# First MLP stage of a transformer block: the last 64 features added by passes of 512 columns over two sums at a time

## The chip, the cores and the metric

The kernel runs on one core of a Trainium2 chip. Its engines work side by side and wait for each other by semaphores: TensorE (PE in the profile; PEld is its weight load) multiplies into the accumulation memory PSUM, VectorE (DVE), ScalarE (ACT) and GpSimd (POOL) work on tiles of 128 partitions, SyncE (SP) issues DMAs. Each engine takes its own instructions in order. The metric is the time of one execution on the device in microseconds; the median of several runs is given.

## The reference

One transformer block with conditioning, two sequences of 2048 tokens with 576 features. The change is in the first product of the MLP, `xn2 @ w1`, and what feeds it.

```python
mod = silu(c) @ w_ada + b_ada
sh_msa, sc_msa, g_msa, sh_mlp, sc_mlp, g_mlp = split(mod, 6, axis=1)
xn = _ln(x, 1e-06) * (1 + sc_msa[:, None, :]) + sh_msa[:, None, :]
q, k, v = heads_of(xn @ w_qkv + b_qkv)          # 16 heads of 36
attn = softmax(einsum('bqhd,bkhd->bhqk', _ln(q), _ln(k)) * 36 ** -0.5)
x = x + g_msa[:, None, :] * (merge(attn @ v) @ w_proj + b_proj)
xn2 = _ln(x, 1e-06) * (1 + sc_mlp[:, None, :]) + sh_mlp[:, None, :]
h = gelu(xn2 @ w1 + b1)                          # 576 -> 2304, exact gelu
out = x + g_mlp[:, None, :] * (h @ w2 + b2)
```

All inputs and outputs are float32.

## The kernel before

The program goes through input products, attention, output products, the first MLP stage, and the second MLP stage. The change is in the first MLP stage and in the preparation of its operands, which is laid between the output products just ahead of it.

The stage works on the 4096 tokens in 8 blocks (`n`) of 512, and on the 2304 hidden features in 9 pairs (`f`) of chunks of 128, one chunk of the left half and one of the right half of `w1`. That makes 72 jobs, numbered job = 9n + f, done two at a time (an even job and the odd one after it). Even jobs use PSUM side 0, odd ones side 1, so a job can begin only when the sums of the job two before it have been read.

Of the 576 features the first 512 are multiplied by a scheme of seven products instead of eight: tokens (two halves t0 and t1 of 256), features (two halves of 256) and hidden chunks (left and right) form a 2 x 2 by 2 x 2 product. `whole_part` issues the seven products m1 to m7 of a job, each two matmuls of 256 columns in float32, which the hardware runs as two passes each: 28 passes. `token_sums` makes the four sums of token parts that the scheme needs, once a block, on VectorE; `weight_sums` makes those of the weights. Six products stand two to a bank in the three PSUM banks of a side (in the order 4, 2, 6, 3, 5, 7), m1 in a bank that the sides share. `hidden_made` combines them: ScalarE copies m1, VectorE does four additions (lines 2121, 2124, 2127, 2128), ScalarE the gelu, GpSimd four sums that the second stage wants, and a DMA stores them.

The last 64 features do not fit the scheme. `last_part` adds them by passes in float32r (one pass instead of two), for which both operands are split into a high part and a rest: the weight tile `wr` has the high parts of 64 rows in partitions 0 to 63 and the rests in 64 to 127, the token tile `parts` has the rows repeated, high in slot 0 and rest in slot 1. Left columns times t0 go to m2, right minus left times t1 to m4, right times t1 to m7, right times t0 to m3: four targets by two slots are eight matmuls of 256 columns a job. `wr` holds three weights: left, right, right minus left.

The token tiles of a block come by DMA from a transposed copy (`turned_loaded`), and ScalarE applies the modulation in place (`turned_modulated`): four operations for the 512 features, then `last_modulated`, which writes the high part (line 393) and the full value into a scratch tile `tail` (line 394), from which GpSimd makes the rest (line 395). `ahead(job)` places this work for the next block between the jobs: tile i of block m+1 is modulated at job 9m + 2i + 2, so its last tile (i = 3) at job 9m + 8. Two tiles of the block after it are normalised and turned at the jobs around it (statistics on lines 277 and 279, turn on line 1042), on VectorE too.

The order on the engines is that of the program text: VectorE, ScalarE, GpSimd, SP and TensorE are told to keep it. In the loop over pairs of jobs it is

```python
ahead(job); whole_part(n0, f0, 0)
if f1 == 0: token_sums(n1)
last_part(n0, f0, 0); ahead(job + 1); hidden_made(n0, f0, 0)
whole_part(n1, f1, 1); last_part(n1, f1, 1)
if f1 == HF - 1 and n1 + 1 < NB: token_sums(n1 + 1)
hidden_made(n1, f1, 1)
```

So where a block begins on an odd job (9, 27, 45, 63) its token sums stand ahead of the additions of the job before, and where it begins on an even job (18, 36, 54) behind those of two jobs before.

Of the kernel before, what the change touches and what calls it, by code (L numbers as in the profile page):

```python
# [12 lines left out]
ALU = mybir.AluOpType  # L13
# [18 lines left out]
def dit_block(  # L32
# [724 lines left out]
    def block_of_small():  # L757
# [294 lines left out]
        def turned_loaded(dst, cols, turned, queue):  # L1052

            full, parts, _ = dst
            queue.dma_start(out=full[:, :, cols], in_=turned[0:512, :].rearrange("(k p) n -> p k n", p=P))
            for r0 in (0, 64):
                queue.dma_start(out=parts[r0 : r0 + 64, 1, cols].bitcast(F32), in_=turned[512:576, :])

        def turned_modulated(dst, cols, which, b):

            full, parts, _ = dst
            for k in range(FULL):
                part = full[:, k, cols]
                nc.scalar.activation(part, part, AF.Identity, **affine(which, k, b))  # L1064
            last_modulated(dst, cols, parts[:, 1, cols].bitcast(F32), which, b)
# [741 lines left out]
        for b in range(B):  # L1807
# [101 lines left out]
            if b + 1 < B:  # L1909
# [68 lines left out]
        wr = [mw.tile([P, MH], F32R, name=f"wr{i}") for i in range(3)]  # L1978
# [14 lines left out]
        for j in range(TPB + 1):  # L1993
            n, t = divmod(j, TPB)
            turned_loaded(xnts[n], slice(t * P, (t + 1) * P), opening["turned"][j], nc.sync)
# [27 lines left out]
        for j in range(TPB + 1):  # L2023
            n, i = divmod(j, TPB)
            due(2 * j + 5, lambda n=n, i=i: turned_modulated(xnts[n], slice(i * P, (i + 1) * P), 2, 0))
# [43 lines left out]
        def sums_of(side):  # L2069

            flat = ps_m[side].rearrange("p b c -> p (b c)")
            return {m: flat[:, i * PAIR : (i + 1) * PAIR] for i, m in enumerate((4, 2, 6, 3, 5, 7))} | {
                1: ps_m1[:, side, :]
            }

        def whole_part(n, f, side):


            a = xnts[n % 2][0]
            t = [slice(0, PAIR), slice(PAIR, BLK)]  # L2080
            moving = {
                1: lambda k: a[:, k, t[0]],
                2: lambda k: a[:, 2 + k, t[0]],
                3: lambda k: ss[4][:, k, :],
                4: lambda k: a[:, 2 + k, t[1]],
                5: lambda k: ss[1][:, k, :],
                6: lambda k: ss[2][:, k, :],
                7: lambda k: a[:, k, t[1]],
            }
            out_m = sums_of(side)  # L2090

            for m in (2, 4, 1, 5, 6, 7, 3) if n == f == 0 else (2, 4, 5, 6, 7, 3, 1):
                for k in range(2):
                    nc.tensor.matmul(  # L2094
                        out_m[m],
                        wb[:, f, slot[m], k, :],
                        moving[m](k),
                        start=k == 0 and m in (1, 2, 5, 6),
                        stop=k == 1 and m == 1,
                    )  # L2100

        def last_part(n, f, side):
            a = xnts[n % 2][1]
            out_m = sums_of(side)

            for m, w, t in ((2, 0, 0), (4, 2, 1), (7, 1, 1), (3, 1, 0)):
                for i in range(2):
                    nc.tensor.matmul(  # L2108
                        out_m[m],
                        wr[w][:, f * P : (f + 1) * P],  # L2110
                        a[:, i, t * PAIR : (t + 1) * PAIR],
                        start=False,
                        stop=i == 1 and m != 2,
                    )

        def hidden_made(n, f, side):
            cs = css[(n * HF + f) % 3]
            flat = ps_m[side].rearrange("p b c -> p (b c)")
            two = lambda i: flat[:, i * PAIR : (i + 2) * PAIR].rearrange("p (a c) -> p a c", a=2)
            nc.scalar.copy(cs[:, 4, :], ps_m1[:, side, :])  # L2120
            nc.vector.tensor_tensor(  # L2121
                cs[:, 0:5:4, :], two(1), cs[:, 4:5, :].to_broadcast([P, 2, PAIR]), ALU.add
            )
            nc.vector.tensor_tensor(
                cs[:, 2:4, :], two(4), cs[:, 4:5, :].to_broadcast([P, 2, PAIR]), ALU.add
            )
            nc.vector.tensor_tensor(cs[:, 1, :], cs[:, 3, :], flat[:, 0:PAIR], ALU.subtract)  # L2127
            nc.vector.tensor_tensor(cs[:, 2:4, :], cs[:, 2:4, :], two(3), ALU.add)  # L2128
# [15 lines left out]
        def ahead(job):  # L2144
# [11 lines left out]
            for what, todo in at(read=0, turn=-2, load=-5, modulate=2):  # L2156
                m, i = todo
                block, cols = xnts[m % 2], slice(i * P, (i + 1) * P)
# [4 lines left out]
                elif what == "read":  # L2163
                    turned_loaded(block, cols, rows_ahead.pop(todo), nc.sync)
                else:
                    turned_modulated(block, cols, 2, m // NBLK)
# [356 lines left out]
```

## Time and profile before

| | |
|---|---|
| median of 3 runs | 3066.44 us (3065.35 to 3068.48) |
| profiled execution | 3067.53 us |
| its span, first to last instruction | 3065.5 us |
| PE busy | 3037.7 us (99%) |
| DVE busy | 1702.6 us (56%) |
| ACT busy | 1497.7 us (49%) |
| POOL busy | 1000.9 us (33%) |
| first MLP stage | from 2112.6 to about 2620 us |

The profile is one execution. Busy time of TensorE is modelled and pipelined, so the rate of its passes is read from start to start in the timeline, not from the mean duration of a record. The share of busy time is an average over stages; the stage of the change has to be read by itself.

### The profile page before, as it was taken

The page shows a single profiled execution, that of the slowest core. Times are in us where ns is not written, and L with a number is a line of the kernel's source. Part 1 is how long each engine was busy: PE and PEld are TensorE (multiplying, and loading weights), DVE is VectorE, ACT ScalarE, POOL GpSimd, SP SyncE. Part 2 cuts the span into 40 slices and gives each one's busy share as a digit, 9 for nine tenths or more (in the row PEclk, how much of TensorE's full clock was granted, in tenths as well). Part 3 has the DMA queues.
Part 4 walks back from the last instruction along what each step waited for, and adds up shares of the span by engine and source line. Part 5 has one row for each costly group of instructions (what it writes and reads, how often), then busy time and mean ns, then how long its engine had stood idle before and what let it go on. Part 6 is the DMA issues. An engine that isn't in the chain of part 4 may idle for free.

```text
span 3065.5 us, 51337 instructions
## 1 busy us (share of the span) xinstructions
PE 3037.7 (99%) x19015; PEld 1891.3 (62%) x19015; DVE 1702.6 (56%) x2614; ACT 1497.7 (49%) x2921; POOL 1000.9 (33%) x1263
## 2 busy tenths in 40 slices
PE   8999999999999999999999999999999999999999
PEld 5884333333333688633333333347888888999999
DVE  6773455444553566544444444447766664667766
ACT  2326666766666223466666666643655553000000
POOL 4651100123222445301101111115545554545444
PEclk9999999999999999999999999999999999999999
DMA  5873322333333454412222222236887887855554
GB/s 146 190 146 93 102 68 71 79 92 93 93 88 94 164 128 81 95 43 69 52 54 72 62 69 66 77 92 191 249 239 238 247 240 279 317 197 193 200 192 157
DMA packets 427939, 415.17 MB, mean 135 GB/s; under 512 B 231472, under 2 KB 355920, under 8 KB 419552
## 3 DMA queue, kind: packets, MB, share of 16 engines
q1 hardware_dynamic: 390824, 314.46, 34.6%
q0 software_dynamic: 36848, 97.33, 11.7%
q8 instruction: 153, 2.51, 0.3%
q14 instruction: 106, 0.87, 0.1%
q10 hardware_dynamic: 8, 0.00, 0.0%
HBM read 246.43 MB, written 154.75 MB: 131 GB/s over the span
## 4 chain that ended last, share of the span: by engine, by line
PE 97%; DVE 1%; DMA 1%; ACT 1%; issue 0%; SPq 0%; POOL 0%; DVEq 0%; ACTq 0%
PE b L1549 30%; PE b L1536 20%; PE b L2353 12%; PE m L2094 11%; PE s L1143 7%; PE s L1229 5%; PE s L1717 4%; PE m L2108 2%; PE one L2094 2%; PE b L2362 2%; PE s L1145 1%; PE s L1235 1%; PE s L1714 1%; DMA xt<-in_x_dram 0%; PE b L197 0%
## 5 line engine op out<-in xcount | busy, mean ns | idle before, releaser
L1540 ACT ACTIVATE pt<-b 128x512 f32<-128x512 f32 x2048 | 1057.4, 608 | 481.7 <-PE b L1549 267.4
L1549 PE MATMUL b<-pt,vt 128*64 128x512 f32 x4096 | 935.0, 598 | 1.8 <-ACT pt L1540 1.8
L1549 PEld LDWEIGHTS b<-pt,vt 128*64 128x64 f32 x4096 | 271.8, 136 | 583.9 <-issue 438.0
L1536 PE MATMUL b<-qm,km 32*128 32x512 f32 x4096 | 563.6, 613 | 0.0
L1605 DVE TENSOR_TENSOR ot<-b,ot 128x512 f32<-128x512 f32 x186 | 128.6, 692 | 549.7 <-PE b L1549 549.7
L1536 PE MATMUL b<-qe,ke 16*128 16x512 f32 x2048 | 420.0, 791 | 0.0
L1536 PEld LDWEIGHTS b<-qm,km 32*128 32x128 f32 x4096 | 190.5, 184 | 271.2 <-ACT pt L1540 210.0
L1143 PE MATMUL s<-wq,xnt 128*128 128x288 f32 x864 | 226.9, 406 | 2.3 <-ACT xnt L400 2.0
L2370 ACT COPY one<-b 128x144 f32<-128x144 f32 x55 | 15.3, 279 | 405.9 <-PE b L2353 405.9
L2094 PE MATMUL m<-xnt,wb 128*128 128x256 f32 x864 | 210.4, 379 | 3.1 <-DVE cs L2128 1.8
L2094 PE MATMUL m<-s,wb 128*128 128x256 f32 x864 | 210.0, 379 | 0.0
L1570 DVE RECIPROCAL den<-den 128x512 f32<-128x512 f32 x62 | 206.8, 3336 | 0.0
L1603 DVE COPY ot<-b 128x512 f32<-128x512 f32 x62 | 42.9, 692 | 262.4 <-PE b L1549 262.4
L1143 PEld LDWEIGHTS s<-wq,xnt 128*128 128x128 f32 x864 | 157.7, 190 | 38.1 <-ACT xnt L400 2.7
L2094 PEld LDWEIGHTS m<-s,wb 128*128 128x128 f32 x864 | 164.2, 190 | 22.4
L1536 PEld LDWEIGHTS b<-qe,ke 16*128 16x128 f32 x2048 | 106.6, 184 | 113.9 <-issue 113.2
L2094 PEld LDWEIGHTS m<-xnt,wb 128*128 128x128 f32 x864 | 158.8, 190 | 23.1 <-DVE cs L2128 2.4
L2132 ACT ACTIVATE cs<-cs,b_sb 128x512 f32<-128x512 f32 x144 | 100.5, 721 | 140.8 <-DVE cs L2127 140.7
L1793 POOL DMA_DIRECT2D spare<-in_x_dram x32 | 17.8, 556 | 453.2 <-DVE met L796 453.2
L2134 POOL TENSOR_TENSOR cs<-cs 128x256 f32<-128x256 f32 x72 | 60.7, 844 | 244.2 <-ACT cs L2132 244.2
L1064 ACT ACTIVATE xnt<-xnt,mod 128x128 f32<-128x128 f32 x244 | 100.0, 481 | 52.7 <-DMA xnt<-turned 45.7
L2121 DVE TENSOR_TENSOR cs<-m,cs 128x512 f32<-128x512 f32 x72 | 49.4, 686 | 136.3 <-PE m L2108 82.4
(369 smaller groups left out, 4583.9 us busy)
## 6 DMA issues: line engine op xcount, KB each, us to landing
operands<-cs SPq DMA_DIRECT2D x70, 896.0 KB
wb<-operands SPq DMA_DIRECT2D x37, 1152.0 KB
operand<-operands SPq DMA_DIRECT2D x19, 1152.0 KB
spare<-in_x_dram POOLq DMA_DIRECT2D x64, 288.0 KB, 3.1
x_dram<-spare POOLq DMA_DIRECT2D x64, 288.0 KB, 2.4
qm<-qk SPq DMA_DIRECT2D x256, 64.0 KB
den<-den_dram SPq DMA_DIRECT2D x124, 128.0 KB
spare<-x_dram POOLq DMA_DIRECT2D x37, 288.0 KB, 3.6
```

The source lines that it names most:

```text
L1064: nc.scalar.activation(part, part, AF.Identity, **affine(which, k, b))
L1143: nc.tensor.matmul(out_a, full[:, k, :], wq[:, k, f], start=k == 0, stop=False)
L1229: nc.tensor.matmul(out[m], x_[:, k, :], w_(k), start=k == 0, stop=k == 1 and m == 6)
L1536: nc.tensor.matmul(ps, k[r, keys], q[r, :], start=first, stop=not first)
L1540: nc.scalar.activation(pt[:, h, :], banks[2 * c + h], AF.Exp, scale=SCALE)
L1549: nc.tensor.matmul(acc[64 * h : 64 * h + 64, :], vt[:, v0 : v0 + 64], pt[:, h, :], start=pt is pts[0][0], stop=pt is pts[-1][0],)
L1570: nc.vector.reciprocal(den[:, part], den[:, part])
L1605: nc.vector.tensor_tensor(ot, acc, ot, ALU.add)
L1717: nc.tensor.matmul(out[m], x_[m][:, k], factors[m][:, k], start=k == 0 and m not in (3, 4), stop=k == 1 and m not in (2, 7),)
L2094: nc.tensor.matmul(out_m[m], wb[:, f, slot[m], k, :], moving[m](k), start=k == 0 and m in (1, 2, 5, 6), stop=k == 1 and m == 1,)
L2132: nc.scalar.activation(part, part, AF.Gelu, bias=b1_sb[:, g : g + 1])
L2353: nc.tensor.matmul(out_m[m], stationary[m][:, c, :], w[:, 7 * c + m - 1, :], start=a == 0 and c == 0, stop=ends and c == FULL - 1 and m no ...
```

## The change

The fourth product gets the opposite sign (its weight sum is `part[2] - part[5]` now), and `hidden_made` adds it where it subtracted it. With that the last 64 features can be added to two neighbours at once: right times (t0 - t1) to m3 and right times t1 to m5; left times t1 to m4 and left times t0 to m2. (m5 enters both outputs of the right chunk; m3, which enters the one for t0 alone, turns right times t1 into right times t0 there.) The products stand in PSUM in the order 4, 2, 3, 5, 6, 7, so that each of these pairs fills a bank of 512 columns, and `last_part` issues two weights by two slots: four matmuls of 512 columns.

The token tile of the tail has three ranges of 256 columns for it: t0 - t1, t1, t0, so that (t1, t0) and (t0 - t1, t1) are each 512 columns in a row. The difference and its two parts are made by a new function, `tails_less`, three VectorE operations of 128 columns a tile, at the modulation of the third and the fourth tile of a block. The scratch tiles `tail` become one tile `tails` for both blocks: one column range each for the first and second tile, one that the third and fourth share. The third weight (right minus left) and the operations that made it go.

```diff
@@ turned_loaded, turned_modulated
-        def turned_loaded(dst, cols, turned, queue):
+        def turned_loaded(dst, cols, turned, queue, ends=None):
...
+            ends = ends or cols
             queue.dma_start(out=full[:, :, cols], in_=turned[0:512, :].rearrange("(k p) n -> p k n", p=P))
             for r0 in (0, 64):
-                queue.dma_start(out=parts[r0 : r0 + 64, 1, cols].bitcast(F32), in_=turned[512:576, :])
+                queue.dma_start(out=parts[r0 : r0 + 64, 1, ends].bitcast(F32), in_=turned[512:576, :])
...
-            last_modulated(dst, cols, parts[:, 1, cols].bitcast(F32), which, b)
+            last_modulated(dst, ends, parts[:, 1, ends].bitcast(F32), which, b)
@@ tiles
-                mx.tile([P, 2, BLK], F32R, name=f"parts{i}"),
-                mx.tile([P, P], F32, name=f"tail{i}"),
+                mx.tile([P, 2, 3 * PAIR], F32R, name=f"parts{i}"),
             )
             for i in range(2)
         ]
+        tails = mx.tile([P, 3 * P], F32, name="tails")
+
+        def block_tile(n, i):
+
+            at = (i + 4) % 6 if i < 2 else i
+            tail = tails[:, min(i, 2) * P : (min(i, 2) + 1) * P]
+            return (*xnts[n % 2], tail), slice(i * P, (i + 1) * P), slice(at * P, (at + 1) * P)
+
+        def tails_less(n, i):
+
+            if i < 2:
+                return
+            cols = slice((i - 2) * P, (i - 1) * P)
+            less, (high, low) = tails[:, cols], (xnts[n % 2][1][:, j, cols] for j in range(2))
+            nc.vector.tensor_tensor(less, less, tails[:, 2 * P :], ALU.subtract)
+            nc.vector.tensor_copy(high, less)
+            nc.vector.tensor_tensor(low, less, high.bitcast(F32), ALU.subtract)
...
-        wr = [mw.tile([P, MH], F32R, name=f"wr{i}") for i in range(3)]
+        wr = [mw.tile([P, MH], F32R, name=f"wr{i}") for i in range(2)]
@@ preparation
-            lambda: nc.vector.tensor_tensor(right, right, left, ALU.subtract),
-            lambda: weight_parts(wr[2], right),
...
-            nc.vector.tensor_tensor(part[6], part[5], part[2], ALU.subtract)
+            nc.vector.tensor_tensor(part[6], part[2], part[5], ALU.subtract)
...
-        for i, t in enumerate((8, 9, 10, 11)):
+        for i, t in enumerate((8, 9)):
             due(t, last_parts[i])
         due(12, lambda: weight_sums(0, 1))
+        due(10, lambda: tails_less(0, 2))
+        due(12, lambda: tails_less(0, 3))
@@ sums_of, whole_part
-            return {m: flat[:, i * PAIR : (i + 1) * PAIR] for i, m in enumerate((4, 2, 6, 3, 5, 7))} | {
+            return {m: flat[:, i * PAIR : (i + 1) * PAIR] for i, m in enumerate((4, 2, 3, 5, 6, 7))} | {
...
-                        stop=k == 1 and m == 1,
+                        stop=k == 1 and m in (1, 7),
@@ last_part
-            for m, w, t in ((2, 0, 0), (4, 2, 1), (7, 1, 1), (3, 1, 0)):
+            for at, w, t in ((0, 0, 1), (2, 1, 0)):
                 for i in range(2):
                     nc.tensor.matmul(
-                        out_m[m],
+                        flat[:, at * PAIR : (at + 2) * PAIR],
                         wr[w][:, f * P : (f + 1) * P],
-                        a[:, i, t * PAIR : (t + 1) * PAIR],
+                        a[:, i, t * PAIR : (t + 2) * PAIR],
@@ hidden_made
-            nc.vector.tensor_tensor(cs[:, 1, :], cs[:, 3, :], flat[:, 0:PAIR], ALU.subtract)
-            nc.vector.tensor_tensor(cs[:, 2:4, :], cs[:, 2:4, :], two(3), ALU.add)
+            nc.vector.tensor_tensor(cs[:, 1, :], cs[:, 3, :], flat[:, 0:PAIR], ALU.add)
+            nc.vector.tensor_tensor(cs[:, 2:4, :], cs[:, 2:4, :], two(2, 3), ALU.add)
@@ ahead
-                    turned_modulated(block, cols, 2, m // NBLK)
+                    turned_modulated(block, cols, 2, m // NBLK, ends)
+                    tails_less(m, i)
```

On TensorE, the end of job 1 and the start of job 2 before the change (m are the products' PSUM tiles, one is m1's, xnt and s hold token parts and their sums, wb the weights of the 512 features; a row's last number counts equal instructions):

```order
L2094 MATMUL one<-xnt_17691,wb 128x256 x2
L2108 MATMUL m_18120<-parts_17692,wr_17700 128x256 x2
L2108 MATMUL m_18120<-parts_17692,wr_17702 128x256 x2
L2108 MATMUL m_18120<-parts_17692,wr_17701 128x256 x4
L2094 MATMUL m_18119<-xnt_17691,wb 128x256 x4
L2094 MATMUL m_18119<-s_18110,wb 128x256 x2
```

And now, at the same place:

```order
L2115 MATMUL one<-xnt_17691,wb 128x256 x2
L2129 MATMUL m_18121<-parts_17692,wr_17699 128x512 x2
L2129 MATMUL m_18121<-parts_17692,wr_17700 128x512 x2
L2115 MATMUL m_18120<-xnt_17691,wb 128x256 x4
L2115 MATMUL m_18120<-s_18111,wb 128x256 x2
```

The eight instructions of 256 columns with three weights have become four of 512 columns with two; nothing else on TensorE moves.

On VectorE, before the change, around job 8, where block 1 is about to begin on job 9 (w_first is work for the second stage, s and xnt the token sums, st to squares the statistics and turn of a later tile, cs<-m the additions of job 8):

```order
L2201 TENSOR_TENSOR w_first<-w_first 128x576
L2064 TENSOR_TENSOR s_18110<-xnt_17694 128x512
L2065 TENSOR_TENSOR s_18111<-s_18110,xnt_17694 128x512
L2066 TENSOR_TENSOR xnt_17694<-xnt_17694 128x2x256
L2067 TENSOR_TENSOR s_18112<-xnt_17694,s_18111 128x512
L277 BN_STATS st<-xt_18106 128x6 x2
L279 BN_AGGR mv<-st 128x2
L283 RECIPROCAL rstd<-std 128x1
L288 TENSOR_SCALAR xt_18106<-xt_18106,mv,rstd 128x576
L1042 STREAM_TRANSPOSE squares<-xt_18106 128x576
L2121 TENSOR_TENSOR cs_18115<-m_18119,cs_18115 128x2x256
```

And now:

```order
L2223 TENSOR_TENSOR w_first<-w_first 128x576
L1989 TENSOR_TENSOR tails<-tails 128x128
L1990 CAST parts_17694<-tails 128x128
L1991 TENSOR_TENSOR parts_17694<-tails,parts_17694 128x128
L2085 TENSOR_TENSOR s_18111<-xnt_17693 128x512
L2086 TENSOR_TENSOR s_18112<-s_18111,xnt_17693 128x512
L2087 TENSOR_TENSOR xnt_17693<-xnt_17693 128x2x256
L2088 TENSOR_TENSOR s_18113<-xnt_17693,s_18112 128x512
L277 BN_STATS st<-xt_18107 128x6 x2
L279 BN_AGGR mv<-st 128x2
L283 RECIPROCAL rstd<-std 128x1
L288 TENSOR_SCALAR xt_18107<-xt_18107,mv,rstd 128x576
```

Three operations of 128 columns, `tails_less` of the block's last tile, stand ahead of the token sums, and so ahead of the statistics and of job 8's additions.

## Rows read from the trace of the kernel before

**Rows 1.** The page's slices: TensorE's granted clock, in tenths of full speed.

```profile
PEclk9999999999999999999999999999999999999999
```

**Rows 2.** The page's chain that ended last, share of the span by engine.

```profile
PE 97%; DVE 1%; DMA 1%; ACT 1%; issue 0%; SPq 0%; POOL 0%; DVEq 0%; ACTq 0%
```

**Rows 3.** Groups by form, TensorE: count | busy us, mean ns | idle us.

```profile
L2108 PE MATMUL m<-parts,wr 128*128 128x256 f32 x576 | 93.9, 306 | 0.0
```

**Rows 4.** Timeline, TensorE, jobs 26 and 27: start us, us, line, tile, count [idle].

```profile
2301.66 1.30 PE L2108 MATMUL m<-parts,wr 128*128 128x256 f32 x8
2302.80 1.89 PE L2094 MATMUL m<-xnt,wb 128*128 128x256 f32 x8
2304.53 1.89 PE L2094 MATMUL m<-s,wb 128*128 128x256 f32 x8
...
2308.66 1.30 PE L2108 MATMUL m<-parts,wr 128*128 128x256 f32 x8
2310.45 1.99 PE L2094 MATMUL m<-xnt,wb 128*128 128x256 f32 x8 [0.49 <-DVE cs L2128]
2312.28 1.89 PE L2094 MATMUL m<-s,wb 128*128 128x256 f32 x8
```

**Rows 5.** Waits of TensorE in the stage: us in total, times, longest.

```profile
PE m L2094 <- DVE cs L2128: 1.8, 3, 0.8
```

**Rows 6.** Timeline, TensorE, query, key and value products.

```profile
98.63 2.10 PE L1143 MATMUL s<-wq,xnt 128*128 128x288 f32 x8
...
109.65 2.10 PE L1143 MATMUL s<-wq,xnt 128*128 128x288 f32 x8
```

**Rows 7.** Timeline, TensorE, end of the output products.

```profile
2094.84 2.10 PE L1717 MATMUL s<-wp,qo 128*128 128x288 f32 x8
2096.78 2.10 PE L1717 MATMUL s<-wp_sums,wb 128*128 128x288 f32 x8
...
2110.19 1.13 PE L1717 MATMUL s<-wp,wb 128*128 128x288 f32 x4
```

**Rows 8.** Groups by form, TensorE, the attention's fp32r passes.

```profile
L1536 PE MATMUL b<-qe,ke 16*128 16x512 f32 x2048 | 420.0, 791 | 0.0
```

**Rows 9.** Timeline, VectorE, ahead of the stage and at its start.

```profile
2099.57 0.74 DVE L405 CAST wr<-spare 64x1152 fp32r<-64x1152 f32 x1
...
2105.55 0.41 DVE L2005 TENSOR_TENSOR wb<-wb 128x256 f32<-128x256 f32 x1
...
2114.53 0.69 DVE L2065 TENSOR_TENSOR s<-s,xnt 128x512 f32<-128x512 f32 x1
```

**Rows 10.** Timeline, VectorE, jobs 26 and 27.

```profile
2301.05 0.72 DVE L2064 TENSOR_TENSOR s<-xnt 128x512 f32<-128x512 f32 x1 [1.21 <-ACT xnt L1064]
2301.88 1.04 DVE L2065 TENSOR_TENSOR s<-s,xnt 128x512 f32<-128x512 f32 x1
2302.85 1.21 DVE L2066 TENSOR_TENSOR xnt<-xnt 128x512 f32<-128x512 f32 x1
2303.98 0.94 DVE L2067 TENSOR_TENSOR s<-xnt,s 128x512 f32<-128x512 f32 x1
2304.84 0.81 DVE L277 BATCH_NORM_STATS2 st<-xt 128x6 f32<-128x288 f32 x2
...
2309.71 0.69 DVE L2128 TENSOR_TENSOR cs<-cs,m 128x512 f32<-128x512 f32 x1
```

**Rows 11.** Timeline, ScalarE, job 26.

```profile
2299.39 1.63 ACT L1064 ACTIVATE xnt<-xnt,mod 128x128 f32<-128x128 f32 x4
...
2301.31 0.48 ACT L394 ACTIVATE tail<-parts,mod 128x128 f32<-128x128 f32 x1
```

**Rows 12.** Timeline, VectorE, job 63.

```profile
2560.29 0.69 DVE L2128 TENSOR_TENSOR cs<-cs,m 128x512 f32<-128x512 f32 x1
```

**Rows 13.** Timeline, TensorE, where job 64 begins.

```profile
2563.29 1.89 PE L2094 MATMUL m<-xnt,wb 128*128 128x256 f32 x8
```

**Rows 14.** Timeline, VectorE, job 24's additions.

```profile
2292.89 0.69 DVE L2128 TENSOR_TENSOR cs<-cs,m 128x512 f32<-128x512 f32 x1
```

More of the change, by code (lines that the diff above doesn't have):

```diff
@@ L1050, in squares_turned, with turned_modulated @@
             return turned
-        def turned_loaded(dst, cols, turned, queue):
+        def turned_loaded(dst, cols, turned, queue, ends=None):
             full, parts, _ = dst
+            ends = ends or cols
             queue.dma_start(out=full[:, :, cols], in_=turned[0:512, :].rearrange("(k p) n -> p k n", p=P))
             for r0 in (0, 64):
-                queue.dma_start(out=parts[r0 : r0 + 64, 1, cols].bitcast(F32), in_=turned[512:576, :])
-        def turned_modulated(dst, cols, which, b):
+                queue.dma_start(out=parts[r0 : r0 + 64, 1, ends].bitcast(F32), in_=turned[512:576, :])
+        def turned_modulated(dst, cols, which, b, ends=None):
             full, parts, _ = dst
+            ends = ends or cols
             for k in range(FULL):
@@ L1994, in block_of_small @@
             n, t = divmod(j, TPB)
-            turned_loaded(xnts[n], slice(t * P, (t + 1) * P), opening["turned"][j], nc.sync)
+            tile, cols, ends = block_tile(n, t)
+            turned_loaded(tile, cols, opening["turned"][j], nc.sync, ends)
         left, right = last_rows[:, 0], last_rows[:, 1]
@@ L2024, in block_of_small @@
             n, i = divmod(j, TPB)
-            due(2 * j + 5, lambda n=n, i=i: turned_modulated(xnts[n], slice(i * P, (i + 1) * P), 2, 0))
-        for i, t in enumerate((8, 9, 10, 11)):
+            tile, cols, ends = block_tile(n, i)
+            due(2 * j + 5, lambda at=(tile, cols, 2, 0, ends): turned_modulated(*at))
+        for i, t in enumerate((8, 9)):
             due(t, last_parts[i])
         due(12, lambda: weight_sums(0, 1))
+        due(10, lambda: tails_less(0, 2))
+        due(12, lambda: tails_less(0, 3))
         places = [
@@ L2103, in last_part @@
             a = xnts[n % 2][1]
-            out_m = sums_of(side)
-            for m, w, t in ((2, 0, 0), (4, 2, 1), (7, 1, 1), (3, 1, 0)):
+            flat = ps_m[side].rearrange("p b c -> p (b c)")
+            for at, w, t in ((0, 0, 1), (2, 1, 0)):
                 for i in range(2):
                     nc.tensor.matmul(
-                        out_m[m],
+                        flat[:, at * PAIR : (at + 2) * PAIR],
                         wr[w][:, f * P : (f + 1) * P],
-                        a[:, i, t * PAIR : (t + 1) * PAIR],
+                        a[:, i, t * PAIR : (t + 2) * PAIR],
                         start=False,
-                        stop=i == 1 and m != 2,
+                        stop=i == 1,
                     )
@@ L2157, in ahead @@
                 m, i = todo
-                block, cols = xnts[m % 2], slice(i * P, (i + 1) * P)
+                block, cols, ends = block_tile(*todo)
                 if what == "load":
@@ L2163, in ahead @@
                 elif what == "read":
-                    turned_loaded(block, cols, rows_ahead.pop(todo), nc.sync)
+                    turned_loaded(block, cols, rows_ahead.pop(todo), nc.sync, ends)
                 else:
-                    turned_modulated(block, cols, 2, m // NBLK)
+                    turned_modulated(block, cols, 2, m // NBLK, ends)
+                    tails_less(m, i)
         at_operand = {1: 0, 2: 2, 3: 4, 4: 3, 5: 5, 6: 6, 7: 1}
```

6 lines of the change are left out of this document (3 added, 3 removed).

## The prediction, made before the changed kernel ran

> **What bounds the kernel now.** I read the page's clock row and the chain that ended last first, then the groups, then the first MLP stage in the timeline and its waits. TensorE runs at its full granted clock all through [rows 1] and owns 97% of the chain [rows 2], so an edit pays only if TensorE has less to do, and costs only if TensorE waits. The edit is in one stage: 72 jobs (8 token blocks by 9 pairs of hidden chunks), whose "last part" is 576 passes, 8 a job [rows 3].
>
> In the timeline the reader is to see a metronome. The last parts of jobs 26 and 27 begin at 2301.66 and 2308.66: 7.00 us a job with no gap [rows 4]. Eight fp32 passes of 256 columns take 2304.53 - 2302.80 = 1.73 us, 0.216 each; a job has 28 of them, 6.05 us. So the eight passes of the last part cost 7.00 - 6.05 = 0.95 us, 0.119 each. (The mean of 306 ns in rows 3 is a pipelined duration and no rate.)
>
> The metronome misses three times: TensorE waited for VectorE's L2128 [rows 5]. Rows 4 show one of them: 2308.66 to 2310.45 is 1.79 us where the job before took 1.14, and the next eight passes take 1.83 instead of 1.73, so 0.75 us are lost. It happens where a new token block begins on an odd job: 9, 27 and 45 (a fourth such place, job 63, does not stall). By the same reading of the three, 1.1 + 0.75 + 0.75 = 2.6 us of the stage are stalls.
>
> **The passes: 8 of 256 columns become 4 of 512.** Columns are the same, 2048 a job; what can go is a cost per pass. At the full granted clock [rows 1], the level of 2.4 GHz, 256 columns at one a cycle are 0.107 us; measured is 0.119, so 12 ns are either per pass or per column. The other fp32r passes tell the two apart: five cycles of eight fp32 and two fp32r passes of 288 columns take 109.65 - 98.63 = 11.02 us, 2.204 each [rows 6]; eight such fp32 passes take 2096.78 - 2094.84 = 1.94 us [rows 7]; so an fp32r pass of 288 columns takes 0.132. The 32 extra columns cost 13 ns, 0.41 ns each: just one a cycle. So the 12 ns belong to the pass, and a pass of 512 columns takes 0.119 + 0.107 = 0.226 us. Four are 0.90, and a job saves 0.95 - 0.90 = 0.05 us, 72 jobs 3.5 us.
>
> The bounds: a 512-column pass can't beat the least that any pass shows over its columns (the fp32 pass of 216 ns, at two cycles a column 213 ns: 3 ns over), so 0.216; then a job saves 0.95 - 0.864 = 0.086, all jobs 6.2 us. If the 12 ns went with the columns, it takes 0.238 and nothing is saved. The only fp32r passes of 512 columns in the trace run four at once on 16 rows each, in the attention [rows 8]; their records overlap so far (791 ns each) that they choose nothing. I take 0.226, since rows 6 tell per pass from per column, and they are the nearest in kind.
>
> The Trainium skill, "TensorE: Matmul & The Clock Gate", section "Back-to-back issue gap", gives the warm gap as columns over 2.4 GHz plus 2.5 ns, for any pass. By it the eight passes would already take 8 x 0.109 = 0.87 us and the change would save only 10 ns a job, 0.7 us in all; the trace differs for fp32r (0.119 and 0.132), and agrees for fp32 if two cycles are counted a column (0.216).
>
> **The three VectorE operations added per second-half token tile (a difference and its two parts, called the trio below).** Seven blocks get theirs inside the stage, two tiles each, 14 trios; the order shows them on VectorE right ahead of the next block's token sums (job 9m+8) or ahead of another tile's statistics (job 9m+6). Price of one: VectorE takes 0.41 us for 256 columns and 0.69 for 512, about 0.27 for 128; the cast of 1152 columns takes 0.74, so 0.25 for 128 is generous [rows 9]; with the hand-overs 0.85 us. The first waits for ScalarE's copy of the tile (L394), the last of six ops of the modulation. Behind it in VectorE's queue stand the token sums, the statistics and turn of a later tile, and then the four additions that free a PSUM side (L2121 to L2128), which TensorE needs two jobs on.
>
> At job 26 this bites. Token sums now start at 2301.05, when the modulation's fourth op is through (2299.39 + 1.63 = 2301.02); L394 runs from 2301.31 to 2301.79 [rows 10, 11]. So the trio starts 0.77 later and ends 0.77 + 0.85 = 1.62 us after the old start of the token sums. Everything behind is serial: token sums, statistics from 2304.84, ScalarE's root, the turn, the four additions, and L2128 is done at 2309.71 + 0.69 = 2310.40, the very moment the stall ends. Part of the 1.62 comes back: beside GpSimd the token sums take 1.04, 1.21 and 0.94 instead of 0.69, 1.1 us lost, and later they meet less of it. From below: all of the 1.1 comes back, +0.5; from above: nothing does and the trio itself runs at the stretched pace (1.21 / 0.69 = 1.75 times), 0.77 + 1.5 = 2.3. I take 1.1, since GpSimd has about 1.2 us of its own work left when the trio begins, which somebody must still wait for. Add 0.1, since TensorE arrives two jobs' saving earlier. So each of the three stalls grows by 1.2 us, 3.6 us in all (1.8 to 7.2).
>
> The Trainium skill, "SBUF — State Buffer", section "SBUF: two separate sides", says VectorE with two SBUF inputs and GpSimd take their shared ports as an exclusive lock for a whole instruction. The stretched token sums agree (1.21 against 0.69 us). By it the trio's cost at a boundary would be 1.62 us less what the lock no longer takes, the sum by my value unchanged.
>
> Elsewhere the trio is covered. At job 63 L2128 ends at 2560.98 and TensorE needs it at 2563.29 [rows 12, 13]: 2.3 us of room for 1.2. At job 24 L2128 ends at 2293.58 [rows 14], TensorE needs it one job before 2302.80, at 2295.80: 2.2 of room, and there statistics follow the trio, so about 0.7 is used. Where a block begins on an even job, the four additions come ahead of the token sums, and nothing is late. If that cover were gone, each of the other eleven trios could cost up to its 0.85.
>
> **At nothing.** Before the stage VectorE loses a subtraction, a cast (0.74 us) and another subtraction of 1152 columns each and gains two trios of 128 [rows 9], while TensorE still has output products to run until 2110.19 + 1.13 = 2111.3 [rows 7]; the last tile's copy on ScalarE now waits for a trio there, but its readers come only in job 0, after that. The turned sign of the fourth sum and the new places of the sums change operands of the same additions, not their number or width. The loads of the tail rows land at other columns; SP's queue has the same DMAs, a few with a wait for TensorE's block before, which is past by then. Removing the third weight copy moves no byte by DMA. None is worth more than 0.3 us together.
>
> **Sum.** Against the profiled execution (3067.53 us, 2.0 beyond its span, and 1.1 above the median 3066.44): -3.5 + 3.6 = +0.1, so 3067.6, or 3066.5 on the scale of the median.
>
> **Rivals.** (a) The per-pass cost sinks to the fp32 floor, since a long pass hides what a short one cannot: 6.2 saved, 3.6 lost, 3063.8. For it: fp32 passes of any width show 3 ns; against: the 288-column pass keeps its 12. (b) The pass cost goes by columns: nothing saved, 3.6 lost, 3070.0; rows 6 speak against it. (c) On the other side, slower: VectorE's queue at jobs 8, 26 and 44 becomes the stage's limit, the trio stretched and nothing regained, 2.4 us a place, 7.2 in all, 3.5 saved: 3070.1. It decides once a trio with its wait takes over 1.3 us net; with the pass cost by columns it is 3073.6. For it: every SBUF op near there is stretched; against: only 1.2 us of GpSimd work is left. (d) The stalls don't grow, because the token sums run free of GpSimd: 3062.9, and with (a) 3060.2. (e) The change doesn't do what it says: the passes stay 8, or the weights are loaded as often. The order shows 4, so I give it no chance of its own.
>
> **Chances.** Forecast 50%, within 3064.5 to 3068.5; (a) 17%, (b) 10%, (c) 13%, (d) 10%. A measurement of this kernel tells about 0.2%, 6.1 us, from no change. Below 3060.3 lies only half of what (d) with (a) can reach, 5%; above 3072.6 the joint of (b) and (c) and stalls at places that I hold covered, 8%; within, 87%. Range 3062.2 to 3070.5: it leaves out the ends of (c) and (d).
>
> **What would show it.** In the changed profile: the last part's group has 288 passes, and the job period is 6.95 us (6.91 by (a), 7.00 by (b)). L2128's equivalent still ends the waits at jobs 9, 27 and 45 and nowhere else, each place losing 1.9 to 2.3 us instead of 0.75 to 1.1 (up to 3.5 by (c), 0.8 by (d)). The trio takes 0.8 to 1.2 us there. I am wrong if the period moves by more than 0.09 us, if other jobs stall, or if the stage before it or after it changes by more than 0.3 us.

## The result and the profile after

| | before | after |
|---|---|---|
| median | 3067.21 us (3065.14 to 3068.86, 8 runs) | 3078.05 us (3073.3 to 3078.66, 8 runs) |
| profiled execution | 3067.53 us, span 3065.5 | 3078.66 us, span 3076.8 |
| job period, start to start | 7.000 us | 6.973 us |
| stalls of the stage, sum | 2.6 us | 13.8 us |

The ratio is 1.0033, 95% interval 1.0024 to 1.0043: slower by a third of a per cent, where 3066.5 and no change were forecast. (A stall is here what the time from one last part to the next has above the period, whatever the reason.)

The passes became what was said: the group of [rows 3] has half the instructions. Columns: count | busy us, mean ns | idle us.

```profile
L2129 PE MATMUL m<-parts,wr 128*128 128x512 f32 x288 | 92.2, 442 | 0.0
```

TensorE's waits in the stage, which answer to [rows 5] (us in total, times, longest):

```profile
PE m L2115 <- DVE cs L2149: 6.1, 4, 1.9
PE m L2115 <- DVE s L2085: 2.2, 3, 1.1
PE m L2115 <- issue: 1.3, 1, 1.3
```

L2149 is the former L2128, L2085 the first token sum, and the third row is the stage's start. The wait for the additions has grown from 1.8 to 6.1 us, and TensorE now waits for the token sums too. TensorE's timeline at jobs 10, 26 to 28 and 46, to be laid beside [rows 4] (start, us, line, tile, count [idle]):

```profile
2186.74 3.68 PE L2115 MATMUL m<-xnt,wb 128*128 128x256 f32 x8 [1.86 <-DVE cs L2149]
2190.22 1.92 PE L2115 MATMUL m<-s,wb 128*128 128x256 f32 x8
...
2298.99 1.28 PE L2129 MATMUL m<-parts,wr 128*128 128x512 f32 x4
2300.11 1.89 PE L2115 MATMUL m<-xnt,wb 128*128 128x256 f32 x8
...
2305.96 1.28 PE L2129 MATMUL m<-parts,wr 128*128 128x512 f32 x4
2307.08 1.89 PE L2115 MATMUL m<-xnt,wb 128*128 128x256 f32 x8
2309.63 1.99 PE L2115 MATMUL m<-s,wb 128*128 128x256 f32 x8 [0.67 <-DVE s L2085]
...
2313.97 1.28 PE L2129 MATMUL m<-parts,wr 128*128 128x512 f32 x4
2317.10 1.99 PE L2115 MATMUL m<-xnt,wb 128*128 128x256 f32 x8 [1.86 <-DVE cs L2149]
2318.93 1.89 PE L2115 MATMUL m<-s,wb 128*128 128x256 f32 x8
...
2323.06 1.28 PE L2129 MATMUL m<-parts,wr 128*128 128x512 f32 x4
...
2445.53 3.08 PE L2115 MATMUL m<-xnt,wb 128*128 128x256 f32 x8 [1.86 <-DVE cs L2149]
```

2305.96 - 2298.99 = 6.97 is the new period. From 2305.96 to 2313.97 it is 8.01, 1.04 too long (the token sums), and from there to the next last part at 2323.06 it is 9.09, 2.12 too long (the additions). Together 3.16 us, where the kernel before lost 0.75.

After the same wait the eight passes from 2186.74 take 3.48 us, those from 2317.10 only 1.83. The windows say why (us, busy time of PE, PEld, DVE, ACT and POOL, then the granted clock, DMA share, GB/s):

```profile
2186.70:2190.20 3.50, 3.46 (x8) 2.77 (x9) 2.30 (x4) 1.43 (x4) 2.61 (x4) 0.52 0.19 29
2316.00:2320.00 4.00, 2.90 (x13) 2.58 (x14) 2.78 (x5) 1.70 (x3) 2.04 (x3) 1.00 1.14 279
2445.50:2449.00 3.50, 3.47 (x10) 2.83 (x11) 2.31 (x4) 1.43 (x4) 2.61 (x4) 0.61 0.14 22
```

At jobs 10 and 46 the granted clock falls to its lower level, 1.2 GHz, for a stretch right behind the wait; each costs 1.7 us more than the same wait at job 28. These stretches are called half-clock stretches below.

The account of the 11.3 us between the two spans: passes 71 x -0.027 = -1.9; the stalls at the three block starts (jobs 9 and 10, 27 and 28, 45 and 46), without what the lower clock adds, 9.65 against 2.60, +7.05; the two half-clock stretches +3.4; a stall of 0.8 at job 69; the stage starts 0.8 later and what follows it takes 1.15 more.

VectorE at jobs 24 and 26, to be laid beside [rows 10] (job 24's trio first, then job 26's and the token sums behind it):

```profile
2292.17 0.41 DVE L1989 TENSOR_TENSOR tails<-tails 128x128 f32<-128x128 f32 x1 [0.33 <-ACT tails L394]
2292.62 0.65 DVE L1990 CAST parts<-tails 128x128 fp32r<-128x128 f32 x1
2293.30 0.71 DVE L1991 TENSOR_TENSOR parts<-tails,parts 128x128 fp32r<-128x128 f32 x1
2293.94 0.80 DVE L277 BATCH_NORM_STATS2 st<-x_first 128x6 f32<-128x288 f32 x2
...
2298.81 0.69 DVE L2149 TENSOR_TENSOR cs<-cs,m 128x512 f32<-128x512 f32 x1
...
2307.53 0.29 DVE L1989 TENSOR_TENSOR tails<-tails 128x128 f32<-128x128 f32 x1 [1.98 <-ACT tails L394]
...
2308.90 0.68 DVE L2085 TENSOR_TENSOR s<-xnt 128x512 f32<-128x512 f32 x1
...
2311.50 0.81 DVE L277 BATCH_NORM_STATS2 st<-xt 128x6 f32<-128x288 f32 x2
...
2316.36 0.69 DVE L2149 TENSOR_TENSOR cs<-cs,m 128x512 f32<-128x512 f32 x1
```

Counted from the start of job 26's last part (2301.66 before, 2305.96 after), the token sums start at -0.61 before and +2.94 after, 3.55 later; the additions end at 8.74 before and 11.09 after, 2.35 later. The 1.2 between is what the token sums won back: from the first to the statistics behind them they take 2.60 us where they took 3.79. And ScalarE, beside [rows 11], jobs 24 to 26:

```profile
2295.39 0.37 ACT L2141 COPY cs<-one 128x256 f32<-128x256 f32 x1
2298.85 1.28 ACT L2153 ACT_TABLE_LOAD   x1 [3.09 <-DVE cs L2148]
2300.15 1.33 ACT L2153 ACTIVATE cs<-cs,b_sb 128x512 f32<-128x512 f32 x2
...
2303.81 1.38 ACT L2153 ACTIVATE cs<-cs,b_sb 128x512 f32<-128x512 f32 x2 [2.07 <-DVE cs L2148]
2305.09 1.64 ACT L1066 ACTIVATE xnt<-xnt,mod 128x128 f32<-128x128 f32 x4
```

The modulation of the next block's last tile (L1066) starts 0.87 us ahead of the last part; before it was 2.27 (2301.66 - 2299.39). So 1.4 us are lost before job 26's own trio begins. The whole stretch from job 24's additions on is a chain without a gap: ScalarE waits 3.09 us for VectorE, loads a table (ACT_TABLE_LOAD; the stage has 27 of them ahead of a square root and 27 ahead of the next gelu), does job 24's gelu, copies m1 of job 25, waits 2.07 us for job 25's additions, does that gelu, and only then modulates.

### The profile page after: what moved, and what is told of

Read it like the earlier page. It is cut to its first block, busy times and chain, and to the rows that moved or that the text cites. A ratio compares the mean times of both kernels' runs of the same rounds, so it can differ in the third digit from the quotient of the medians.

```text
span 3076.8 us, 50806 instructions
## 1 busy us (share of the span) xinstructions
PE 3040.8 (99%) x18727; PEld 1878.1 (61%) x18727; DVE 1718.9 (56%) x2659; ACT 1495.5 (49%) x2921; POOL 994.3 (32%) x1263
## 4 chain that ended last, share of the span: by engine, by line
PE 95%; DMA 2%; DVE 1%; ACT 1%; issue 0%; POOL 0%; SPq 0%; DVEq 0%; ACTq 0%; POOLq 0%
PE b L1551 30%; PE b L1538 20%; PE b L2375 12%; PE m L2115 10%; PE s L1145 7%; PE s L1231 5%; PE s L1719 4%; PE b L2384 2%; PE m L2129 2%; PE one L2115 2%; PE s L1147 1%; DMA operands<-cs 1%; PE s L1237 1%; PE s L1716 1%; DMA xt<-in_x_dram 0%
## 5 line engine op out<-in xcount | busy, mean ns | idle before, releaser
L1066 ACT ACTIVATE xnt<-xnt,mod 128x128 f32<-128x128 f32 x244 | 100.0, 481 | 52.4 <-DMA xnt<-turned 52.4
```

## The experiments

Fourteen kernels ran. All are edits of the changed kernel but one, and are judged by the median and by the profile's stalls. "Modulation" is the start of L1066 ahead of job 26's last part. Where a kernel leaves a trio out, the range that the trio writes is filled once ahead of the stage and keeps old values.

**1. The trios or the passes?** First the changed kernel without the trios in the stage:

```diff
                     turned_modulated(block, cols, 2, m // NBLK, ends)
-                    tails_less(m, i)
```

> The changed kernel without the trios inside the stage (the third range of the tail tile keeps old values, so that part of the product is left out); four passes of 512 columns stay. Theory (lateness adds up): the two trios of a block delay one serial chain of VectorE and ScalarE, and TensorE waits at jobs 9, 27 and 45. Without them the three stalls fall back to 2.6 us in all, the job period stays at 6.97 us, and the time is 1.9 us under the kernel before: about 3065. Rival (long passes): the wider passes themselves free the PSUM side later, so the stalls of some 14 us stay: about 3076. Rival (my prediction's price): only the trio ahead of the token sums counts; same as the theory here.

Measured: 3066.39 us, ratio 0.9996 (0.9987 to 1.0006). Stalls 2.8 us, no half clock, modulation at 2.27 again. Then the changed kernel with the old 256-column passes:

```diff
+                    for h in range(2):
-                        flat[:, at * PAIR : (at + 2) * PAIR],
+                        flat[:, (at + h) * PAIR : (at + h + 1) * PAIR],
-                        a[:, i, t * PAIR : (t + 2) * PAIR],
+                        a[:, i, (t + h) * PAIR : (t + h + 1) * PAIR],
```

> The changed kernel with its last part issued as eight passes of 256 columns again (same targets, weights and values), trios as they are. Theory (lateness adds up): stalls stay near 14 us, the job period goes back to 7.00 us, so 1.9 us above the changed kernel: about 3080. Rival (long passes): the stalls vanish with the wide passes: about 3067.

Measured: 3078.01 us, ratio 1.0032 (1.0022 to 1.0042), period 7.000, stalls 12.9 us. Its waits:

```profile
PE m L2115 <- DVE cs L2150: 5.5, 3, 1.8
PE m L2115 <- DVE s L2085: 1.8, 3, 0.9
```

The trios are the whole loss. The passes' gain shows in the period (7.000 against 6.973) but not in the time: the two kernels with trios differ by less than their runs do, since the stalls differ too.

**2. Which trio?** Only the third tile's (jobs 9m + 6), and only the fourth's (9m + 8):

```diff
-                    tails_less(m, i)
+                    if i == 2:
+                        tails_less(m, i)
```

> The changed kernel with, inside the stage, only the third tile's trio of each block (job 9m+6); the fourth tile's is left out, so part of the product is. Theory (lateness adds up): the trio delays the statistics, ScalarE's root and the additions behind it, and two jobs later ScalarE's modulation starts some 1.4 us later against TensorE; each of the three stalls grows by about that: 2.6 + 4 = 7 us, time about 3070. Rival (my prediction): that trio is covered, the stalls stay at 2.8 us and the time at 3066.

> The changed kernel with, inside the stage, only the fourth tile's trio of each block (job 9m+8), right ahead of the token sums; the third tile's is left out, so part of the product is. Theory (lateness adds up): the copy's wait (0.77 us) and the trio (about 1.4 us beside GpSimd) less 1.2 us that the token sums get back, 1.0 us a place: stalls 2.6 + 3 = 5.6, time about 3069. Rival (my prediction with its upper bound): this trio alone makes the 11 us without the half clock, about 3074.

Measured: third alone 3072.12 us (ratio 1.0013, 1.0004 to 1.0022), stalls 8.6 us with one half-clock stretch of 1.7; fourth alone 3069.84 (1.0008, 0.9999 to 1.0017), stalls 6.0 us. Less the 2.8 us of the kernel without trios, and the half clock, that is 4.1 and 3.2 us; the sum is 7.2 by the unrounded stalls, and the changed kernel's block starts have 7.05 over before. So the trio that had been priced, the fourth tile's, costs what was forecast, and the one held covered costs more. ScalarE with the third alone:

```profile
2295.69 1.28 ACT L2157 ACT_TABLE_LOAD   x1 [3.09 <-DVE cs L2152]
2296.99 1.34 ACT L2157 ACTIVATE cs<-cs,b_sb 128x512 f32<-128x512 f32 x2
...
2301.95 1.65 ACT L1066 ACTIVATE xnt<-xnt,mod 128x128 f32<-128x128 f32 x4
```

Its job 26 has the last part at 2302.80: modulation 0.85 ahead, the 1.4 us of the changed kernel. With the fourth alone it is 2.27.

**3. Why had the third trio no room?** In the kernel before, ScalarE's table load for job 24's gelu stood ahead of the wait for VectorE, and there was an idle 1.04 us ahead of the next copy:

```profile
2289.68 1.28 ACT L2132 ACT_TABLE_LOAD   x1
2292.89 1.44 ACT L2132 ACTIVATE cs<-cs,b_sb 128x512 f32<-128x512 f32 x2 [1.92 <-DVE cs L2127]
2295.37 0.37 ACT L2120 COPY cs<-one 128x256 f32<-128x256 f32 x1 [1.04 <-DMA turned<-squares]
```

In the rows above the load stands behind the wait. The order of the instructions with their waits shows the same, before and after the change (a name in brackets is the engine or DMA queue that is waited for):

```
L2120 COPY cs_18113<-one 128x256 [waits DMAHW3_49,PE_49]
L2132 ACT_TABLE_LOAD
L2132 ACTIVATE cs_18113<-cs_18113,b_sb 128x512 [waits DVE_49] x2

L2141 COPY cs_18114<-one 128x256 [waits DMAHW3_49,PE_49,Pool_49]
L2153 ACT_TABLE_LOAD [waits DVE_49]
L2153 ACTIVATE cs_18114<-cs_18114,b_sb 128x512 [waits Activation_49]
```

Of the 27 table loads for the gelu, 10 waited for VectorE before and 19 do now. The kernel without trios and the one with the short passes have 19 too, so the move needs neither the trios nor the long passes. An operation of one column that needs the gelu's table and waits for nothing puts the load ahead again:

```diff
             nc.scalar.copy(cs[:, 4, :], ps_m1[:, side, :])
+            if n * HF + f in (6, 24, 42):
+                nc.scalar.activation(spot[:, 0:1], b1_sb[:, 0:1], AF.Gelu)
```

In the changed kernel, and in the one with the third trio alone:

> The changed kernel with one more ScalarE operation of one column at jobs 6, 24 and 42: a gelu on a spot tile between the copy of m1 and the job's own gelu. It waits for nothing, so ScalarE's table load (1.28 us), which in the changed kernel stands behind the wait for job 24's additions (298.85 in the trace, right ahead of the gelu at 2300.15) and in the kernel before stood ahead of that wait (2289.68), comes early again. Theory A, the third tile's trio alone: its lateness of about 1.5 us is carried whole to the modulation of job 26; the load is nothing: modulation 0.9 us ahead of job 26's last part as in the changed kernel, stalls of the stage 13 to 14 us with two half-clock stretches, median 3078 (3073 to 3079). Theory B, trio and load together: the load behind the wait had used up the 1.0 us that ScalarE had idle there before, so the trio found no room; with the load early the modulation comes 2.0 to 2.3 us ahead of the last part, the three places stall as with the fourth tile's trio alone (6.0 us in all, perhaps 1 more), no half clock, median 3070 (3068.5 to 3072).

> The same early table load at jobs 6, 24 and 42 in the kernel that makes the third tile's three operations only (the fourth tile's range keeps old values from the second block on). Theory A: as that kernel without it, stalls 8.6 us, modulation 0.85 us ahead of job 26's last part, median 3072. Theory B: stalls 2.8 to 3.8 us, modulation 2.0 to 2.3 us ahead, no half clock, median 3066.4 to 3067.5.

Measured: 3070.27 us (ratio 1.0012, 1.0003 to 1.0021), stalls 6.2 us, no half clock; and 3067.01 (0.9998, 0.9989 to 1.0007), stalls 3.1 us. ScalarE of the first:

```profile
2291.43 0.35 ACT L2142 COPY cs<-one 128x256 f32<-128x256 f32 x1
2291.80 1.28 ACT L2144 ACT_TABLE_LOAD   x1
2293.09 0.20 ACT L2144 ACTIVATE spot<-b_sb 128x1 f32<-128x1 f32 x1
2295.07 1.39 ACT L2156 ACTIVATE cs<-cs,b_sb 128x512 f32<-128x512 f32 x2 [1.77 <-DVE cs L2151]
...
2300.07 1.64 ACT L1066 ACTIVATE xnt<-xnt,mod 128x128 f32<-128x128 f32 x4
```

With its last part at 2302.19 the modulation is 2.12 ahead. So theory B holds: the moved load alone costs nothing, the third trio alone costs 0.3 us (3.1 - 2.8), both together 4.1 us and a half-clock stretch. The load used up the room that the trio needed. The kernel without trios has the load behind the wait too, and modulates at 2.27 all the same:

```profile
2291.86 1.28 ACT L2156 ACT_TABLE_LOAD   x1 [3.27 <-DVE cs L2151]
```

What moved the wait can be read from the orders in part. In both programs the load stands behind the wait exactly where the copy of m1 waits for GpSimd too; the gelu then waits for two engines, ScalarE itself and VectorE, where elsewhere it waits for VectorE alone. At the nine jobs that are new, among them 6, 24 and 42, ScalarE's write of the scratch range just before (L394) waited for GpSimd and no longer does. That points to the scratch tile that both blocks now share, but no kernel with only that undone was run.

The Trainium skill, "ScalarE: Activation LUTs", section "What ACT_TABLE_LOAD costs", gives about 1283 ns for a load and 2.66 us for a switch with a drain. The trace agrees on the load (1.28 us) and shows no drain: in the changed kernel the gelu starts 1.30 us after the load does (2298.85, 2300.15), and in the rows just shown the load starts 0.02 us after the copy ahead of it has ended (2291.43 + 0.35).

**4. Another engine, another place.** The trios on GpSimd, and on VectorE behind the work that TensorE waits for:

```diff
-        def tails_less(n, i):
+        def tails_less(n, i, engine=nc.gpsimd):
...
-            nc.vector.tensor_tensor(less, less, tails[:, 2 * P :], ALU.subtract)
+            engine.tensor_tensor(less, less, tails[:, 2 * P :], ALU.subtract)
...
```

> The changed kernel with the trios inside the stage on GpSimd in place of VectorE. Theory (lateness adds up): VectorE's queue no longer waits for ScalarE's last copy, so the stalls fall to 2.6 us plus what VectorE loses beside 1.4 us more of GpSimd work, at most 0.7 a place: 3065 to 3067. Rival (long passes): about 3076. Rival (any trio): GpSimd's sums and stores come later by a trio and stall the stage in other jobs: 3070 or more.

```diff
-                    tails_less(m, i)
+                    later[i] = lambda m=m, i=i: tails_less(m, i)
...
                     token_sums(n1)
+                    run_later(3)
...
                 hidden_made(n0, f0, 0)
+                run_later(2)
```

> The changed kernel with the third tile's trio behind the additions of its job and the fourth tile's trio behind the token sums, both still on VectorE. Theory (lateness adds up): the third tile's trio then delays nothing that the boundary waits for, the fourth costs its 0.85 us once per place and no wait for the copy; each stall 0.75 to 1.1 plus 0.9, 5 us in all, no half clock: about 3068. Rival (my prediction's price, the order of the two does not matter): the stalls fall only by the 0.77 us of the copy's wait each, to some 11 us: about 3075.

Measured: 3066.06 us (0.9998, 0.9988 to 1.0007), stalls 3.1; and 3069.17 (1.0006, 0.9997 to 1.0016), stalls 6.0, of them 0.5 at job 69. GpSimd has the room (it is 32% busy over the span of the changed kernel, and 33% with the trios). Behind the token sums the fourth trio still stands ahead of the additions, and still costs; for the third, behind the additions of its job, no cost is left to see, since the sum is no more than with the fourth alone.

**5. The price of a pass.** The last part issued twice, in the kernel with the trios on GpSimd:

```diff
-            for at, w, t in ((0, 0, 1), (2, 1, 0)):
+            for at, w, t, more in ((0, 0, 1, True), (2, 1, 0, True), (0, 0, 1, False), (2, 1, 0, False)):
...
```

> The kernel with the trios on GpSimd, its last part issued twice in every job (so the last 64 features count twice in the output). The job period less 6.973 us is the price of four passes of 512 columns in the middle of a run of such passes. If the cost over one cycle a column goes by the pass (my prediction): 4 x 0.226 = 0.90, period 7.88. If it goes by the column: 4 x 0.238 = 0.95, period 7.93. At the fp32 floor: 0.86, period 7.84.

```profile
2299.51 2.21 PE L2129 MATMUL m<-parts,wr 128*128 128x512 f32 x8
...
2307.41 2.20 PE L2129 MATMUL m<-parts,wr 128*128 128x512 f32 x8
```

One run, 3129.7 us. The period is 7.90 and no job stalls: (7.895 - 6.973) / 4 = 0.2305 us a pass of 512 columns, between the 0.226 forecast and the 0.238 by columns.

**6. The stall that was there before.** With the trios on GpSimd the three old stalls remain. Here the next block's statistics and turn are laid behind the additions where a block begins on an odd job, and the same is done to the kernel before:

```diff
+                if f1 == 0:
+                    hidden_made(n0, f0, 0)
                 ahead(job + 1)
-                hidden_made(n0, f0, 0)
+                if f1:
+                    hidden_made(n0, f0, 0)
```

> Trios on GpSimd, and where a block begins on an odd job the additions of the job before it stand ahead of the later tile's statistics and turn instead of behind them. Theory: the three stalls that are left (3.1 us) go, since the additions then end 2 us or more before TensorE needs the side; job period 6.97: about 3063. Rival: the turn, now later, holds up the next additions or the reads of the next tile, and the stall moves to the jobs after: about 3066.

> The kernel before with only that exchange (additions ahead of statistics and turn where a block begins on an odd job). Theory: its three stalls of 2.6 us go: about 3064.5. Rival: they move to the jobs after: 3067.

Measured: 3065.22 us (0.9993, 0.9984 to 1.0002), stalls 2.3; and 3066.79 (1.0000, 0.9992 to 1.0009), stalls 1.7. The old stalls are gone, but new ones came at jobs 13, 14 and 50, as the rivals said. Since VectorE also makes the second stage's weight sums there, these were taken from the jobs 10, 28 and 46, in three ways (one kernel each, in this order):

```diff
-                for _ in range(2):
-                    if job >= 2 and making_weights:
+                for _ in range(2):
+                    if job >= 2 and job not in (10, 28, 46) and making_weights:
...
+                for _ in range({10: 0, 28: 0, 46: 0, 14: 4, 60: 4}.get(job, 2)):
...
+                for _ in range({10: 0, 28: 0, 46: 0, 14: 4, 56: 4, 58: 3}.get(job, 2)):
```

> The kernel with the trios on GpSimd and the additions ahead of the turn, and in the pairs of jobs that follow an odd boundary (10, 28, 46) no work for the second stage's weights on VectorE (it is done in later pairs). Theory (VectorE and ScalarE are one serial chain there, and each op on it is late once for all): the stalls at jobs 13, 14 and 50 (2.3 us) go, stage 495.1 us, about 3063. Rival: the stalls come from ScalarE's table loads and the reads of the next tile alone, and stay: 3065.

> As the version that spares VectorE the weight work after odd boundaries, but with that work caught up at the pairs of jobs 14 and 60, so that the second stage's first weights are asked for some 28 us earlier than there. Theory: the stage keeps its 495.6 us (stalls 0.4) and the second stage starts without a wait: about 3063 to 3064, under the kernel before and the one with the turn behind. Rival: the heavier pairs at 14 and 60 stall in their turn, 3065 or more; or the weights are late still, over 3070.

> As the version before it, but the spared weight work is caught up at the pairs of jobs 14 and 56 (whose extra steps issue nothing on VectorE or one load) and one step at 58, so that the second stage's first weights are asked for at job 64, as in the kernel before. Theory (what stalled at job 70 were those loads, put late in SP's queue ahead of a store): no stall at job 70, stalls in the stage under 1 us, about 3063 to 3064. Rival (the stall at job 70 came from VectorE's heavier pairs): it stays, over 3068.

Measured: 3078.05 (1.0036, 1.0022 to 1.0051), 3071.6 (1.0014, 1.0005 to 1.0023) and 3063.41 (0.9986, 0.9977 to 0.9995). The first has a stage nearly without stalls (0.4 us), as forecast, and pays at its end, which was not: there the second stage's weights are late:

```profile
PE b L2378 <- DMA operand<-operands: 6.6, 1, 6.6
PE b L2378 <- DMA w_first<-w_kept: 3.8, 1, 3.8
```

The second wasn't faster either: it stalls at job 70, for ScalarE, which itself waited 13.9 us for a DMA by the profile:

```profile
PE one L2115 <- ACT cs L2141: 5.7, 1, 5.7
```

The third does the missed work by job 58. From 2040 to 2700 us TensorE waits for nothing in the stage beyond its start (L1719 is the stage before):

```profile
PE m L2115 <- issue: 1.3, 1, 1.3
PE s L1719 <- DVE spare L1607: 0.8, 1, 0.8
```

Its stage, from the first last part to the last, takes 495.4 us against 499.6 of the kernel before and 508.9 of the changed one. It beats both, by 3.8 and 14.6 us. Of the 4.2 us against the kernel before, 1.9 are the passes, so the gain that was forecast for them is there in part once nothing stalls.

## Why the prediction was wrong

**"Elsewhere the trio is covered": this step failed.** For job 24 it said 2.2 us of room and 0.7 used. TensorE indeed doesn't wait there: the additions end at 2299.50 and are needed at 2300.11, where TensorE begins job 26. But 1.6 us of the room were used, not 0.7: the trio itself took 1.77 us there (2292.17 to 2293.94) where 0.85 was reckoned. And room against TensorE wasn't the question. VectorE and ScalarE hand their lateness on, through two gelus and a copy, to the modulation two jobs later, where the block starts and no room is left. Experiment 2 gives the size, 4.1 us without the half clock, and experiment 3 the cause: the trio together with a table load of 1.28 us that the change moved behind a wait, neither of them alone. The moved load was in the order of the changed program, but only in ScalarE's waits, and the prediction read that order for TensorE and VectorE. Nor was it weighed, under "At nothing", that the new scratch tile could change who waits for whom.

**The fourth tile's trio: mechanism right, the size by luck.** Forecast +3.6 us at jobs 9, 27 and 45, measured +3.2 alone. Two terms were off and nearly cancel: 2.15 us lost ahead of the token sums instead of 1.62, since the trio takes 1.42 us (the three means below) in the stage's mean and not 0.85, and 1.2 us won back instead of 0.5. Means of the 14 trios (busy us, mean ns | idle us):

```profile
L1989 DVE TENSOR_TENSOR tails<-tails 128x128 f32<-128x128 f32 x14 | 7.1, 510 | 21.9 <-ACT tails L394 21.9
L1990 DVE CAST parts<-tails 128x128 fp32r<-128x128 f32 x14 | 7.1, 505 | 0.5
L1991 DVE TENSOR_TENSOR parts<-tails,parts 128x128 fp32r<-128x128 f32 x14 | 5.7, 407 | 0.5
```

The token sums as a wait of their own were not foreseen. They add nothing: 1.04 and 2.12 at jobs 27 and 28, 3.16 in all, are the old 0.75 and the 2.4 by which the additions are later, taken in two parts.

**The passes: mechanism right, size off.** -1.9 us instead of -3.5. The 12 ns above one column a cycle were given to the pass, from a step of 32 columns that the rows could hardly resolve; the step of 256 takes 0.2305 - 0.119 = 0.1115 us, some 5 ns over the 0.107 of one column a cycle, so about two fifths of the 12 ns go with the columns. The Trainium skill, "TensorE: Matmul & The Clock Gate", section "Back-to-back issue gap", has the formula that the prediction quotes (columns over 2.4 GHz plus 2.5 ns), but for a single pass by itself, not for any pass. It would put 0.216 us on this one; measured in a run of such passes is 0.2305, and here the measurement decides.

**The half clock: not in the sum.** [Rows 1] showed a full clock all through, and no cost stood for losing it. Two of the three longer waits brought it, 3.4 us.

**Rivals.** (c) had the sign, and nearly the size of the stalls, 7.2 us against 7.05, for another reason: it put the whole on the trios of jobs 8, 26 and 44, with nothing won back. The runs give these 3.2, with 1.2 us a place won back, and the rest to jobs 6, 24 and 42, so its size was near by luck. (d) and (a) are excluded, (b) holds for about two fifths of the 12 ns. (e) is excluded. Of what was to show the forecast wrong, the stage's start and what follows it moved by 0.8 and 1.15 us. The first last part begins at 2118.6 before and 2119.4 after, and anywhere from 2116.5 to 2119.3 in the other kernels, which are nearly alike up to there, so the 0.8 is no effect of the passes. What follows the last of them takes 447.3 us before, 448.5 after and 448.9 with the short passes, so that isn't either; its cause stays open. The 0.8 us at job 69 come with a copy on ScalarE that waits 7.85 us for a DMA by the profile, and experiment 4 shows the same stall with less lateness; its cause was not isolated.

## What to carry to other kernels

Room against the bottleneck engine is not enough to call work covered: follow the late instruction along its own engine, and the engines that it feeds, to the next place where work is due, and see whether anything idles between. When tiles are merged or split, read the waits of every engine anew, since a wait that moves ahead of a table load (1.28 us here) uses up room that other work may need. And give such small work to the engine that has room: on GpSimd these trios cost nothing that could be measured.

## What the hardware showed unexpectedly

- A wait of TensorE of about 2 us (2.12 us above the period) was followed by a granted clock of 0.52 and 0.61 at two places, and of 1.00 at the third. Each of the two cost 1.7 us, nearly as much as the wait. What tells the three apart stays open. It isn't the job: with the third trio alone a wait of 1.85 us was followed by 0.51 at job 28 and by 1.00 at job 10, and with the fourth alone one of 1.87 us at job 10 by 1.00.
- The period is 6.973 us in ten kernels with the long passes and 6.987 in the two of experiment 3, an unexplained 1 us over the stage.
- The three operations of 128 columns on VectorE take from 0.29 to 0.80 us in the stage. The last of them (L1991) takes 0.29 us in the seven of its 14 runs that no work of GpSimd overlaps, 0.44 in five that it overlaps in part, and 0.72 in two that it covers. On GpSimd itself the two subtractions take 0.60 and 0.48 us in the mean.
